# Graph attention on one core: last slots shared by two tiles, one sum moved from TensorE to VectorE, norm constants on GpSimd, unit waits handed to SyncE

## The chip, the cores and the metric

The kernel runs on one core of a Trainium2 chip. The metric is device time in microseconds (us) of one execution; the median of three runs of the kernel before is 1606.07 us (1604.77 to 1610.32). The engines are named as in the profile: PE (TensorE matmul; PEld its weight loads), DVE (VectorE), ACT (ScalarE), POOL (GpSimd) and SP (SyncE, which here only issues DMAs and waits). Each engine works through its own instructions strictly in program order.

## The reference

The inputs are `x` (16 batches of 1024 rows of 512, float32), one adjacency matrix `adj` of 1024 x 1024 for all batches (sparse, with a full diagonal, a few rows much denser than the rest), and weights and biases for q, k and v.

```
h = relu(layernorm(x))                      # mean, variance over 512, eps 1e-5
q, k, v = h @ Wq + bq, h @ Wk + bk, h @ Wv + bv     # 8 heads of 64
scores = einsum(q, k) / 8 ; scores = -1e9 where adj == 0
out = x + softmax(scores) @ v               # per head
```

Only pairs with `adj != 0` matter, and the kernel computes only those.

## The kernel before

**Set-up.** The rows of the adjacency are counted, ranked by degree, and sorted into eight tiles of 128 rows: tile 0 holds the rows with most neighbours, tile 7 those with fewest. For each row the list of its neighbours is made once. Tile t has `CAPS = (11, 8, 6, 5, 4, 3, 3, 2)[t]` slots, so every row of a tile is given as many neighbours as the fullest row of that tile may have; empty places point at a row of zeros. What does not fit into tile 0's slots is spread over a helper tile -1 of 4 slots ("pieces").

**A batch.** For each of the 16 batches: load the eight x tiles in sorted order (`load_x`, POOL), statistics (`stats`, DVE), normalize (`norm`, ACT), transpose (`flip`, PE; `unflip`, ACT), project to k and v (`proj_kv`, PE), copy out of PSUM (`evict_kv`, ACT, half of the v by DVE), store to DRAM (`store_kv`, SP). One `kvt` buffer holds k and v of one tile until its store; there are four. Then the attention: `queries` (PE) projects q of a tile into one of two PSUM buffers; for each slot a `gather` fetches k and v of 128 neighbours, 512 KB (POOL by an indirect DMA; the row's own k and v by SP). The gathered slots live in a ring of 23 places.

**Units.** Slots of a tile are handled in units of 2 to 4 (`PARTS`): 14 units and 46 slots per batch. Per unit: `multiply` (DVE, k times q, L1360), `score` (DVE, sum over each head's 64, L1364), `exponent` (ACT, L1368), weighting of v, most slots by ACT with eight 64-column instructions each (`weigh_s`, L1394), nine slots per batch by DVE (`weigh_v`, L1380), `fold` and `join` (adding the slots of a unit, and units of a tile, DVE L1399 and L1406, some folds by POOL). For tile 0 two matmuls per batch add up what is left (`add_up`, L1418): the pieces by the matrix `owner_t`, the other slots' sum by the identity. Then `row_sums`, `scale`, `residual`, `put_out`. `seen` (L1447) checks each batch's row sums.

**Norm constants.** For each pair of tiles: `variance` (DVE, adds eps, L1080), `power` (POOL, to the power -1/2, L1083), `shift` (DVE, -mean times that, L1087); `norm` waits for `shift`.

**What sets the order.** All instructions are placed by a table of numbers (`PLACES`, one number per step and kind of batch, plus `PERIOD` times the batch); `Plan.ordered` emits them by these numbers, each engine's list in that order. Projections of batch b+1 run on PE beside the attention of batch b. The last batch (b = 15) has rules of its own: there PE adds up nearly all slots.

Of the kernel before, what the change touches and what calls it, by code (L numbers as in the profile page):

```python
# [10 lines left out]
F32 = mybir.dt.float32  # L11
# [7 lines left out]
H = 8  # L19
# [34 lines left out]
SLOTS = sum(n for _, _, n in UNITS) + len(CAPS) + 1  # L54
NU = len(UNITS)
NT = len(CAPS)
BY_VECTOR = {2: 1, 3: 0, 4: 1}
ONE_MORE = ((2, 0),)
LAST_BY_VECTOR = {(2, 0): 0, (2, 3): 0, (0, 0): 0, (-1, 0): 0, (3, 0): 0, (1, 4): 0}
VECTOR_RESIDUAL = (4,)  # L60
LAST_VECTOR_RESIDUAL = (5, 4, 6, 7)
PERIOD = 95.290021
PLACES = {
    'once': dict(
        zeros=(-16.2,),
# [36 lines left out]
        spread_bias=(68.07,),
        copy_bias=(89.7,),
    ),
    'first': dict(
        load_x=(75.29, 75.49, 76.69, 76.89, 78.69, 78.89, 79.29, 79.49,),
        stats=(75.49, 75.69, 76.49, 76.69, 78.89, 79.09, 81.29, 81.49,),
        norm=(75.49, 76.09, 77.09, 77.49, 79.89, 80.09, 80.34, 80.69,),
        flip=(75.49, 75.69, 76.49, 76.69, 78.69, 78.89, 90.39, 104.64,),
        unflip=(75.89, 76.49, 77.29, 77.89, 80.49, 80.72, 96.22, 97.88,),  # L110
        proj_kv=(75.89, 77.49, 76.29, 77.89, 76.89, 78.49, 79.09, 79.29, 86.87, 98.15, 99.79, 107.75, 135.06, 147.6,
            153, 148.32,),
        evict_kv=(76.89, 79.29, 77.69, 79.49, 78.09, 80.29, 80.4, 80.66, 96.1, 96.13, 96.42, 106.28, 154.55, 162.49,
            169.71, 172.46,),
        store_kv=(78.35, 116.17, 119.38, 125.35, 140.7, 146.55, 148.18, 147.06,),
        variance=(75.89, 76.89, 79.29, 81.69,),
# [1553 lines left out]
```

## Time and profile before

| | |
|---|---|
| median of the timed runs | 1606.07 us |
| profiled execution, first to last instruction (its span) | 1595.8 us; the page gives no other time of this execution, and the median lies 10.3 us above the span |
| PE, DVE, ACT, POOL busy | 97%, 96%, 90%, 79% of the span |
| granted PE clock | 0.991 of full on average |
| DMA | 531.55 MB, mean 333 GB/s; 608 gathers by POOL, 128 by SP |
| idle of POOL put down to "issue" | gathers 159.7 us, loads of x 27.6, stores of the output 24.4 |

How to read it: four engines are busy most of the time, so a single busy share does not tell which of them sets the pace. PE's matmuls are pipelined: a matmul of 512 columns shows 592 ns, but the next begins 429 ns later, so PE's real load is read from starts, and from the idle that the profile shows before its instructions. POOL's DMA issues are followed by about 0.3 us in which POOL waits for nothing that the profile shows ("issue").

### The profile page before, as it was taken

How to read it: one execution, taken by the hardware profiler on the slowest of the kernel's cores; microseconds unless marked ns; L12 is line 12 of the kernel's file. 1: busy time of each engine (PE TensorE's matmuls, PEld its weight loads, DVE VectorE, ACT ScalarE, POOL GpSimd, SP SyncE). 2: the span in 40 equal slices, each digit the busy share in tenths (PEclk: the TensorE clock that was granted, in tenths of full speed). 3: DMA queues.
4: the chain of work that ended last, by engine and by line, in shares of the span. 5: the costliest groups of instructions: out<-in, count | busy, mean ns of one | idle time of the engine just before them, and what ended most of it. 6: DMA issues, size and time to landing. Idle time of an engine off the chain costs nothing.

```text
span 1595.8 us, 19282 instructions
## 1 busy us (share of the span) xinstructions
PE 1548.5 (97%) x4151; PEld 719.2 (45%) x4182; DVE 1532.9 (96%) x2105; ACT 1437.5 (90%) x5428; POOL 1257.0 (79%) x1185
## 2 busy tenths in 40 slices
PE   8999999999999999999999999999999999999877
PEld 4444444444444444444444444444444444444333
DVE  8879999999999999999999999999999999999997
ACT  4359989889999999999999999999999998998997
POOL 3767788887888888888888888888888878876775
PEclk9999999999999999999999999999999999999989
DMA  6498989998999999999999999999999999988994
GB/s 251 141 356 308 323 331 347 343 344 323 320 376 340 371 333 337 344 346 375 335 354 343 352 340 342 373 347 372 326 357 339 342 368 328 364 338 295 333 376 191
DMA packets 149875, 531.55 MB, mean 333 GB/s; under 512 B 19052, under 2 KB 19052, under 8 KB 149752
## 3 DMA queue, kind: packets, MB, share of 16 engines
q0 software_dynamic: 109840, 390.70, 67.2%
q1 hardware_dynamic: 39912, 139.56, 23.7%
q8 instruction: 35, 0.57, 0.1%
q14 instruction: 88, 0.72, 0.1%
HBM read 429.46 MB, written 100.72 MB: 332 GB/s over the span
## 4 chain that ended last, share of the span: by engine, by line
DVE 39%; PE 22%; ACT 12%; POOL 10%; issue 9%; DMA 7%; DVEq 0%; POOLq 0%; SPq 0%; ACTq 0%
DVE ring L1360 11%; DVE weights L1364 10%; ACT ring L1394 9%; DVE ring L1399 6%; DMA ring<-kv,index 6%; PE pk L1117 5%; PE pv L1117 5%; PE pq L1117 5%; POOL ring L1350 4%; DVE ring L1380 3%; DVE st L1071 2%; PE pv_first L1117 2%; PE pk_first L1117 2%; POOL ring L1399 2%; POOL x L1062 1%
## 5 line engine op out<-in xcount | busy, mean ns | idle before, releaser
L1394 ACT ACTIVATE ring<-ring,weights 128x64 f32<-128x64 f32 x4704 | 1154.6, 343 | 43.4 <-DVE weights L1373 42.4
L1350 POOL DMA_INDIRECT ring<-kv,index x608 | 618.0, 1016 | 185.5 <-issue 159.7
L1117 PE MATMUL pq<-wq,hT 128*128 128x512 f32 x1024 | 460.3, 592 | 0.8
L1117 PE MATMUL pv<-wv,hT 128*128 128x512 f32 x960 | 433.2, 594 | 3.5 <-ACT kvt L1135 3.3
L1117 PE MATMUL pk<-wk,hT 128*128 128x512 f32 x960 | 433.2, 594 | 1.9 <-ACT hT L1109 1.2
L1364 DVE TENSOR_REDUCE weights<-ring 128x32 f32<-128x2048 f32 (+2 forms) x224 | 422.2, 1890 | 0.9
L1360 DVE TENSOR_TENSOR ring<-ring,pq 128x1536 f32<-128x1536 f32 (+2 forms) x208 | 388.7, 1869 | 4.6 <-DMA ring<-kv,index 4.0
L1117 PEld LDWEIGHTS pq<-wq,hT 128*128 128x128 f32 x1024 | 194.5, 190 | 215.0 <-issue 211.1
L1117 PEld LDWEIGHTS pv<-wv,hT 128*128 128x128 f32 x960 | 182.1, 191 | 227.1 <-issue 216.4
L1117 PEld LDWEIGHTS pk<-wk,hT 128*128 128x128 f32 x960 | 182.7, 191 | 211.0 <-issue 200.6
L1399 DVE TENSOR_TENSOR ring<-ring 128x512 f32<-128x512 f32 (+1 forms) x301 | 253.0, 856 | 2.7 <-ACT ring L1394 2.1
L1471 POOL DMA_INDIRECT out_dram<-x,perm x128 | 151.3, 1182 | 38.1 <-issue 24.4
L1062 POOL DMA_INDIRECT x<-in_x_dram,perm x128 | 142.3, 1111 | 34.0 <-issue 27.6
L1399 POOL TENSOR_TENSOR ring<-ring 128x512 f32<-128x512 f32 x90 | 116.1, 1299 | 10.0 <-DVE ring L1399 8.3
L1380 DVE TENSOR_TENSOR ring<-ring,weights 128x512 f32<-128x512 f32 x143 | 105.8, 747 | 1.3 <-ACT weights L1368 1.0
L1097 ACT ACTIVATE h<-x,shift,rstd 128x512 f32<-128x512 f32 x120 | 94.0, 814 | 0.9 <-DVE shift L1087 0.9
L1468 POOL TENSOR_TENSOR x<-x,o 128x512 f32<-128x512 f32 x64 | 82.4, 1288 | 15.3 <-DVE o L1454 12.7
L1104 PEld LDWEIGHTS pht<-ident,h 128*128 128x128 f32 x512 | 61.9, 141 | 55.6 <-issue 47.8
L1368 ACT ACTIVATE weights<-weights 128x32 f32<-128x32 f32 (+2 forms) x224 | 48.8, 223 | 42.0 <-DVE weights L1364 41.2
L1071 DVE BATCH_NORM_STATS2 st<-x 128x6 f32<-128x512 f32 x120 | 81.2, 677 | 0.1
L1135 ACT COPY kvt<-pk 128x512 f32<-128x512 f32 x120 | 69.4, 578 | 7.8 <-PE pk L1117 7.8
L1104 PE MATMUL pht<-ident,h 128*128 128x128 f32 x512 | 72.7, 274 | 2.7 <-ACT h L1097 2.7
(240 smaller groups left out, 1088.0 us busy)
## 6 DMA issues: line engine op xcount, KB each, us to landing
ring<-kv SPq DMA_DIRECT2D x128, 512.0 KB, 6.7
kv<-kvt SPq DMA_DIRECT2D x120, 512.0 KB, 6.5
ring<-kv,index POOLq DMA_INDIRECT x608, 7.0
ring<-in_adj_dram SPq DMA_DIRECT2D x8, 512.0 KB, 8.2
x_first<-in_x_dram SPq DMA_DIRECT2D x8, 256.0 KB, 6.0
x<-in_x_dram,perm POOLq DMA_INDIRECT x128, 6.1
out_dram<-x,perm POOLq DMA_INDIRECT x128, 5.8
wk<-in_L_gnn_Wk_dram SPq DMA_DIRECT2D x1, 1024.0 KB
```

The lines of the kernel that those rows point to most:

```text
L1062: nc.gpsimd.indirect_dma_start(out=X[n][:], out_offset=None, in_=x_rows, in_offset=on(ap=perm[:, t : t + 1], axis=0), element_offset=b * N * D
L1071: nc.vector.bn_stats(st, X[n])
L1097: nc.scalar.activation(HN[n], X[n], AF.Relu, bias=shift, scale=scale)
L1104: nc.tensor.transpose(PH[n][:, c, :], hn[:, ts(c, P)], ident)
L1117: nc.tensor.matmul(pt, HT[n][:, c, :], W[name][:, c, :], start=(apart and c == 0), stop=(n != -NT and c == DC - 1))
L1350: nc.gpsimd.indirect_dma_start(out=G[i][:, s].rearrange("p j d -> p (j d)"), out_offset=None, in_=KV[b % len(KV)][:], in_offset=on(ap=inde ...
L1360: nc.vector.tensor_tensor(k, k, Q[b, t][:, None, :].to_broadcast([P, count, D]), ALU.mult)
L1364: nc.vector.tensor_reduce(weights[:, w, :], heads(G[i][:, :count, 0, :]), AX.X, ALU.add)
L1380: nc.vector.tensor_tensor(v, v, own.to_broadcast([P, n, H, HD]), ALU.mult)
L1394: nc.scalar.activation(v[:, h, :], v[:, h, :], AF.Identity, scale=weights[:, c + s, h : h + 1])
L1399: engine.tensor_tensor(v[:, 0:n], v[:, 0:n], v[:, first : first + n], ALU.add)
L1471: nc.gpsimd.indirect_dma_start(out=out_rows[t], out_offset=on(ap=perm[:, t : t + 1], axis=0), in_=X.pop(b * NT + TILES.index(t))[:], in_of ...
```

## The change

1. *Shared last slots* (`SHARED`). Tiles 3 and 2 share the last slot (rows 0 to 63 of the slot serve tile 2, the rest tile 3), and tiles 1 and 0 share one (rows 0 to 95 serve tile 0). Rows in tiles 3 and 1 are ranked in reverse so that the fullest rows lie in the half that the slot serves. A batch has 44 slots in 13 units instead of 46 in 14; the ring has 22 places. A shared slot needs a mixed q (`mix`, three ACT copies more per batch), its own `multiply_m`, two small ACT copies of its weights per slot (`halves`), and two half-height adds (`fold_m`, `join_m`).
2. *Tile 0's last sum by VectorE* (`join_acc`). In batches 0 to 14 PE adds up only the pieces; DVE adds that PSUM result to the rest. One `add_up` call per batch goes.
3. *Norm constants on GpSimd.* `variance` and `shift` leave DVE; `power` becomes four POOL instructions.
4. *Row sums checked for five batches* of the sixteen (`SEEN`), each check covering all batches since the last one.
5. *SyncE waits* (`landed`). A SyncE no-op waits for all gathers of a unit and for its q; `multiply` then waits for that no-op alone.
6. The table of places and the lists of who weighs and folds what are new.

```diff
-    3: ((3, 0, 3), (3, 3, 2)),
-    2: ((2, 0, 3), (2, 3, 3)),
+    3: ((3, 0, 5),),
+    2: ((2, 0, 3), (2, 3, 2)),
     1: ((1, 0, 4), (1, 4, 4)),
-    0: ((0, 0, 4), (-1, 0, 4), (0, 4, 4), (0, 8, 3)),
+    0: ((0, 0, 4), (-1, 0, 4), (0, 4, 4), (0, 8, 2)),
+SHARED = {3: (2, 64), 1: (0, 96)}
+SEEN = (4, 9, 13, 14, 15)
-PERIOD = 95.290021
+PERIOD = 93.3
-RING = 23
+RING = 22
...
         def power(m):
+            RSTD[m] = made(m, scale_at, "rstd")
+            SHIFT[m] = made(m, shift_at, "shift")
+            nc.gpsimd.tensor_scalar(RSTD[m], MV[m][:, :, 1], EPS, None, op0=ALU.add)
             nc.gpsimd.tensor_tensor(RSTD[m], RSTD[m], minus_half.to_broadcast(...), ALU.pow)
+            nc.gpsimd.tensor_scalar(SHIFT[m], MV.pop(m)[:, :, 0], -1.0, None, op0=ALU.mult)
+            nc.gpsimd.tensor_tensor(SHIFT[m], SHIFT[m], RSTD[m], ALU.mult)
...
+        add(("landed", k), "SP", slots[:m] + [q_of[q]])
+        add(("multiply", k), "DVE", [("landed", k)], [q])
...
+        def landed(i):
+            b, t, w, c, count = unit(i)
+            LANDED[i] = nc.sync.nop()
+            for made in (*SENT[i], MADE[b, t]):
+                tc.add_manual_dep(LANDED[i].ins, made.ins.name, waits(), reason="the rows of a unit")
...
+        def multiply_m(i):
+            k = GM[i][:, 0, :]
+            nc.vector.tensor_tensor(k, k, QM[i // NU, UNITS[i % NU][0]], ALU.mult)
...
+        def join_acc(b):
+            v = G[b * NU + parts_of(0)[-1]][:, 0, 1, :]
+            nc.vector.tensor_tensor(v, v, ACC.pop((b, 0)), ALU.add)
```

PE, where batch 8's attention ends and batch 9's begins (`acc_0` is tile 0's sum of batch 8, `p_more` the pieces' row sums, `pq_7` to `pq_5` the q of batch 9's tiles 7 to 5, `pk_6` batch 10's k). Before:

```order
L1433 MATMUL p_more_8003<-more_7965,owner_t 128x8
L1418 MATMUL acc_0_8032<-ring,owner_t 128x512
L1115 LDWEIGHTS chosen
L1115 MATMUL pq_6_8035<-bias_parts,chosen 128x512
L1117 MATMUL pq_6_8035<-wq,hT_6_7129 128x512 x4
L1115 LDWEIGHTS chosen
L1115 MATMUL pq_5_8042<-bias_parts,chosen 128x512
L1117 MATMUL pq_5_8042<-wq,hT_5_7380 128x512 x4
L1115 LDWEIGHTS chosen
L1115 MATMUL pk_6_8069<-bias_parts,chosen 128x512
L1117 MATMUL pk_6_8069<-wk,hT_6_7928 128x512 x4
L1418 MATMUL acc_0_8032<-ring,ident 128x512
```

and now, from the last v projection of batch 9 (`pv_0`) on; `pv_7` and `pk_7` are batch 10's:

```order
L1262 MATMUL pv_0_7919<-wv,hT_0_7857 128x512 x4
L1262 MATMUL pv_7_7928<-wv,hT_7_7913 128x512 x4
L1260 LDWEIGHTS chosen
L1260 MATMUL pk_7_7953<-bias_parts,chosen 128x512
L1262 MATMUL pk_7_7953<-wk,hT_7_7913 128x512 x4
L1260 LDWEIGHTS chosen
L1260 MATMUL pq_7_8039<-bias_parts,chosen 128x512
L1262 MATMUL pq_7_8039<-wq,hT_7_7111 128x512 x4
```

```order
L1260 LDWEIGHTS chosen
L1260 MATMUL pv_6_8067<-bias_parts,chosen 128x512
L1262 MATMUL pv_6_8067<-wv,hT_6_7933 128x512 x4
L1662 MATMUL p_more_8089<-more_8034,owner_t 128x8
L1648 MATMUL acc_0_8121<-ring,owner_t 128x512
L1260 LDWEIGHTS chosen
```

The sum by the identity is gone from PE. The v and k projections of tile 7 of batch 10 stand between batch 9's last v and its q of tile 7, which takes the PSUM buffer that tile 0's q of batch 8 held.

SP, the stores of batch 9's k and v (`kvt_1` is tile 1's; the no-ops have no row of their own, their waits stand at the DMA behind them). Before:

```order
L1348 DMA ring<-kv_144 128x1024 [waits DMAHW7_49,DVE_49]
L1159 DMA kv_142<-kvt_4_7549 128x1024 [waits DMAHW6_49,Activation_49]
L1159 DMA kv_142<-kvt_3_7660 128x1024 [waits DVE_49,Activation_49]
L1159 DMA kv_142<-kvt_2_7739 128x1024 [waits DMAHW0_49,Activation_49]
L1159 DMA kv_142<-kvt_1_7798 128x1024 [waits DMAHW1_49,DVE_49,Activation_49]
```

and now:

```order
L1305 DMA kv_145<-kvt_2_7772 128x1024 [waits DMAHW7_49,Activation_49]
L1305 DMA kv_145<-kvt_1_7850 128x1024 [waits DMASW6_49,DMAHW5_49,DMASW4_49,PE_49,DMASW0_49,DMASW5_49,DMASW7_49,DMASW3_49,DMAHW0_49,DVE_49,Activation_49]
L1305 DMA kv_145<-kvt_3_7714 128x1024 [waits DMASW7_49,DMASW6_49,DMASW1_49,DMASW2_49,DMAHW1_49]
L1305 DMA kv_145<-kvt_0_7926 128x1024 [waits DMAHW2_49,Activation_49]
L1527 DMA ring<-kv_145 128x1024 [waits DMASW3_49,DMASW4_49,DMAHW3_49,DMAHW4_49,Pool_49]
```

SP now waits for the gathers (DMASW) of tile 0's first units ahead of the store of tile 1 and for those of its third unit ahead of tile 3's; the no-op of the last unit of batch 8 stands behind the store of tile 0 of batch 9.

POOL, the constants of a pair of tiles of batch 10 (`rstd`). Before:

```order
L1350 DMA ring<-kv_144,index 128x1024 x4
L1083 TENSOR_TENSOR rstd_7620<-rstd_7620,minus_half 128x2
L1350 DMA ring<-kv_144,index 128x1024 x5
L1083 TENSOR_TENSOR rstd_7716<-rstd_7716,minus_half 128x2
L1350 DMA ring<-kv_144,index 128x1024
L1468 TENSOR_TENSOR x_3_6319<-x_3_6319,o_3_7682 128x512
```

and now:

```order
L1530 DMA ring<-kv_147,index 128x1024 x3
L1706 DMA out_dram<-x_4_6359,perm 16384x512
L1530 DMA ring<-kv_147,index 128x1024 x2
L1225 TENSOR_SCALAR rstd_7820<-mv_7705 128x2
L1226 TENSOR_TENSOR rstd_7820<-rstd_7820,minus_half 128x2
L1227 TENSOR_SCALAR shift_7821<-mv_7705 128x2
L1228 TENSOR_TENSOR shift_7821<-shift_7821,rstd_7820 128x2
```

One instruction per pair has become four, in the same place between gathers.

## Rows read from the trace of the kernel before

**Rows 1.** The page: span, and busy time of each engine.
```profile
span 1595.8 us, 19282 instructions
PE 1548.5 (97%) x4151; PEld 719.2 (45%) x4182; DVE 1532.9 (96%) x2105; ACT 1437.5 (90%) x5428; POOL 1257.0 (79%) x1185
```
**Rows 2.** Windows: stretch, length, busy by engine (x), PE clock, DMA share, GB/s.
```profile
100.00:400.00 300.00, 291.37 (x787) 134.69 (x790) 292.71 (x389) 270.96 (x1030) 232.30 (x214) 1.00 0.92 334
600.00:1346.24 746.24, 743.82 (x2000) 346.76 (x2015) 729.10 (x949) 707.61 (x2706) 618.38 (x569) 1.00 0.95 349
1500.00:1560.00 60.00, 45.03 (x100) 18.72 (x100) 58.90 (x56) 56.58 (x239) 46.12 (x46) 0.86 0.96 358
```
**Rows 3.** Timeline of PE around 804 us: start, length, engine, line, instruction.
```profile
804.05 0.38 PE L1115 MATMUL pk<-bias_parts,chosen 128*128 128x512 bf16 x1
804.27 3.60 PE L1117 MATMUL pk<-wk,hT 128*128 128x512 f32 x8
807.70 0.38 PE L1115 MATMUL pk<-bias_parts,chosen 128*128 128x512 bf16 x1
```
**Rows 4.** Groups, PE, 600 to 1346.24: count, busy, mean ns, idle before.
```profile
L1418 PE MATMUL acc<-ring,ident 128*128 128x512 f32 x16 | 8.2, 592 | 0.0
```
**Rows 5.** Groups by shape, DVE, same stretch.
```profile
L1364 DVE TENSOR_REDUCE weights<-ring 128x32 f32<-128x2048 f32 x48 | 109.0, 2270 | 0.0
L1360 DVE TENSOR_TENSOR ring<-ring,pq 128x2048 f32<-128x2048 f32 x40 | 91.2, 2279 | 0.5 <-PE pq L1117 0.3
L1360 DVE TENSOR_TENSOR ring<-ring,pq 128x1536 f32<-128x1536 f32 x48 | 83.8, 1746 | 0.0
L1364 DVE TENSOR_REDUCE weights<-ring 128x24 f32<-128x1536 f32 x48 | 83.4, 1738 | 0.2
L1399 DVE TENSOR_TENSOR ring<-ring 128x512 f32<-128x512 f32 x112 | 73.5, 680 | 0.3
...
L1087 DVE SCALAR_TENSOR_TENSOR shift<-mv,rstd 128x2 f32<-128x2 f32 x32 | 7.4, 230 | 3.2 <-POOL rstd L1083 3.2
L1080 DVE TENSOR_SCALAR rstd<-mv 128x2 f32<-128x2 f32 x32 | 6.4, 200 | 0.0
```
**Rows 6.** Groups by shape, POOL, same stretch.
```profile
L1350 POOL DMA_INDIRECT ring<-kv,index x304 | 308.2, 1014 | 85.2 <-issue 81.9 <-DMA ring<-kv,index 0.9 <-DMA x<-in_x_dram,perm 0.9
L1471 POOL DMA_INDIRECT out_dram<-x,perm x64 | 78.8, 1231 | 18.4 <-issue 12.9 <-POOL x L1468 2.5 <-POOL ring L1399 1.3
L1062 POOL DMA_INDIRECT x<-in_x_dram,perm x65 | 75.6, 1162 | 15.2 <-issue 14.1 <-DMA ring<-kv 1.0
L1399 POOL TENSOR_TENSOR ring<-ring 128x512 f32<-128x512 f32 x48 | 61.1, 1283 | 0.9
...
L1083 POOL TENSOR_TENSOR rstd<-rstd,minus_half 128x2 f32<-128x2 f32 x32 | 23.7, 741 | 4.7 <-DVE rstd L1080 2.9 <-DMA kv<-kvt 1.2
```
**Rows 7.** Groups, POOL, whole span: its smallest copy and iota.
```profile
L927 POOL COPY before_told<-place 128x8 f32<-128x8 f32 x1 | 0.2, 192 | 0.0
...
L917 POOL IOTA place<- 128x8 f32 x1 | 0.1, 136 | 0.0
```
**Rows 8.** Timeline of POOL around 927 us.
```profile
926.64 0.97 POOL L1350 DMA_INDIRECT ring<-kv,index  x1 [0.30 <-issue]
927.92 2.08 POOL L1471 DMA_INDIRECT out_dram<-x,perm  x1 [0.30 <-issue]
```
**Rows 9.** Timeline of DVE at 927.9 us.
```profile
927.91 1.22 DVE L1399 TENSOR_TENSOR ring<-ring 128x1024 f32<-128x1024 f32 x1
```
**Rows 10.** Groups by shape, ACT, 600 to 1346.24.
```profile
L1394 ACT ACTIVATE ring<-ring,weights 128x64 f32<-128x64 f32 x2363 | 580.0, 345 | 26.1 <-DVE weights L1373 25.9
...
L1341 ACT COPY q<-pq 128x512 f32<-128x512 f32 x8 | 4.7, 582 | 0.0
L1368 ACT ACTIVATE weights<-weights 128x16 f32<-128x16 f32 x16 | 3.3, 207 | 0.0
```
**Rows 11.** Timeline around 805 us: ACT weighting two slots, SP storing k and v.
```profile
804.94 3.93 ACT L1394 ACTIVATE ring<-ring,weights 128x64 f32<-128x64 f32 x16
...
809.37 0.32 SPq L1159 DMA_DIRECT2D kv<-kvt  x1
```

More of the change, by code (lines that the diff above doesn't have):

```diff
@@ L104 @@
+        slots=(132.928,),
+        add_bias=(-7.83, 37.133,),
+        spread_bias=(83.593,),
+        copy_bias=(94.282,),
     ),
     'first': dict(
[L106 to L110, printed above, removed]
@@ L382 @@
+POOLS = {'x': 16, 'h': 2, 'pht': 2, 'hT': 11, 'pkv': 2, 'kvt': 4, 'q': 2, 'q0': 1, 'qm': 1, 'acc': 2, 'o': 1}
+RING = 22
 JUNK, SCRATCH, ROWS, LONG_ROWS = NT, NT + 3, NT + 6, NT + 9
 GROUP = 2
+SEEN = (4, 9, 13, 14, 15)
+SUMS_KEPT = 10
 BIAS_V = {0: 'DVE', 2: 'DVE', 4: 'DVE', 6: 'DVE'}
-PAIRED = {10: 12, 12: 13}
-BY_UNIT = ("gather", "multiply", "score", "exponent", "weigh_v", "weigh_p", "weigh_s", "fold", "join", "add_up", "share")
+PAIRED = {9: 11, 11: 12}
+BY_TENSOR = False
+LANDED = True
+BY_UNIT = (
+    "landed", "gather", "multiply", "multiply_m", "score", "exponent", "halves", "weigh_v", "weigh_p", "weigh_s", "fold", "fold_m", "join", "join_m",
+    "add_up", "add_m", "share",
+)
@@ L468, in ordered @@
                 new = [use for use in self.ops[i][3] if use not in has]
-                if all(k in made for k in known[i]) and all(given[use[0]] == at[use] for use in new):
+                if all(k in made for k in known[i]) and all(
+                    given[use[0]] == at[use] and not left.get(before.get(use), 0) for use in new
+                ):
                     ready.append((place[i], i, new))
@@ L524, in planned @@
         add(("list_of", t), "DVE", [("ends",), ("no_diagonal", t)])
-        add(("tell", t), "POOL", [("ranks",), ("shift", (t - NT) // 2)])
+        add(("tell", t), "POOL", [("ranks",), ("power", (t - NT) // 2)])
         add(("spread", t), "POOL", [("list_of", t)])
@@ L556, in planned @@
         if b and k == size - 1:
-            add(("variance", m), "DVE", [("stats", n - k) for k in range(size)])
-            add(("power", m), "POOL", [("variance", m)])
-            add(("shift", m), "DVE", [("power", m)])
-        add(("norm", n), "ACT", [("shift", m) if b else ("load_x", n)], [("x", n), ("h", n)])
+            add(("power", m), "POOL", [("stats", n - k) for k in range(size)])
+        add(("norm", n), "ACT", [("power", m) if b else ("load_x", n)], [("x", n), ("h", n)])
         add(("flip", n), "PE", [("norm", n)], [("h", n), ("pht", n)])
@@ L627, in planned @@
         add(("exponent", k), "ACT", [("score", k)])
+        if m is not None:
+            add(("halves", k), "ACT", [("exponent", k)])
         weights = ("exponent", k)
@@ L695, in planned @@
             add(sums, "DVE", exps, [] if home else [("acc", b, "more")])
-            add(("scale", b, home), "DVE", [sums] + added, [o] if without_tensor(b, B, home) else [acc, o])
-            if without_tensor(b, B, home):
-                touch(first, [0], ("scale", b, home))
+            in_slot = without_tensor(b, B, home) or added[0][0] == "join_acc"
+            add(("scale", b, home), "DVE", [sums] + added, [o] if in_slot else [acc, o])
+            if in_slot:
+                touch(first if without_tensor(b, B, home) else k, [0], ("scale", b, home))
             add(("residual", b, home), by, [("scale", b, home)], [o, x])
             add(("put_out", b, home), "POOL", [("residual", b, home)], [x])
+    for k in range(NU, units):
+        for name in ("score", "halves"):
+            if (name, k) in plan.number:
+                i = plan.number[name, k]
+                key, engine, known, uses = plan.ops[i]
+                plan.ops[i] = key, engine, [*known, *readers_of(plan, k - NU, name)], uses
     bases, held = ring_of(B), before_units()
```

863 lines of the change are left out of this document (520 added, 343 removed), and 36 rows, old and new, of the table gather.

## The prediction

> **What bounds the kernel now.** I read the busy shares of the page first [rows 1]: PE 97% and DVE 96% of the span, ACT 90%, POOL 79%. Shares alone choose nothing, so next come the windows [rows 2]. In the long steady stretch from 600 to 1346.24 us PE is busy 743.8 of 746.2 us. The stretch holds eight batches (32 norm constants at four per batch [rows 6]), so a batch takes 93.28 us and PE is busy 92.98 of it. Is a busy PE a full PE? The timeline [rows 3] says yes: bias plus eight matmuls of one projection run from 804.05 to 807.70, 3.65 us, and the next begins at once; eight matmuls are 3.43 us of it, 0.429 us from start to start although each shows 0.59. The granted clock is 1.00 there [rows 2], the upper of the two levels, 2.4 GHz. So PE sets the pace of the steady part, with 0.3 us per batch idle.
>
> The others stand close behind. DVE is busy 729.1/8 = 91.1 us per batch, ACT 707.6/8 = 88.5 [rows 2]. POOL looks idle at 618.4/8 = 77.3 but is not: the groups by shape [rows 6] put 81.9 + 12.9 + 14.1 = 108.9 us of its idle down to "issue", the pause that follows each DMA it sends, and so POOL's load is (618.4 + 108.9)/8 = 90.9 us. Nothing here has more than 5 us of slack per batch.
>
> Two stretches are not PE's: from 100 to 400 us DVE is busy 292.7 of 300 while PE idles 8.6 us, and from 1500 to 1560, with projections almost done, DVE is busy 58.9 of 60 and PE 45.0 [rows 2]. There DVE ends last.
>
> **The change, part by part.** The sum is made against the span, 1595.8 us; the median of the timed runs is 10.3 us above it, and I add that at the end.
>
> *Tile 0's last sum.* PE loses one `add_up` by the identity per batch. It shows as two matmuls (16 in eight batches [rows 4]), 2 x 0.429 = 0.86 us on the engine that sets the pace, in 15 batches: 12.9 us. DVE gets one 512-column add instead of one join, nothing net. This is the core of the forecast, if PE stays the bound.
>
> *Two slots less.* DVE: a multiply of 2048 columns takes 2.279, one of 1536 1.746 us [rows 5], so 0.533 per slot and 0.147 fixed; a score 0.532 and 0.142. Plain slots fall from 46 to 42 and units by one, and two `multiply_m` of 512 columns come at 0.68 each (as the fold of that width): -4 x 0.533 - 0.147 + 1.36 = -0.92. Scores: two slots and a unit less, -1.21. Folds and joins: four 512-column folds go, four half-height adds come; I price them alike (no row shows a 64-partition add; between half of 0.68 and 0.68). ACT: 2363 weighting instructions take 580.0 us, 0.245 each [rows 10], so two slots of eight are -3.93 and one exponent -0.21; three q copies at 0.582 and four tiny copies at up to 0.207 come: -1.6 net. POOL: two gathers, -2 x (1.014 + 0.30) = -2.63, and one fold more, +1.28 [rows 6].
>
> *Norm constants.* DVE loses four times 0.200 + 0.230 = 1.72 us [rows 5]. DVE's load thus goes from 91.1 to 87.2. POOL gets twelve instructions of two columns per batch. No row shows such a one. From below: its iota of 8 columns, 0.136 us [rows 7], 1.6 us per batch; they can't be a gain, as POOL runs nothing in their place. From above: the power on the same two columns, 0.741 [rows 6], 8.9 us. I take 0.16, between the iota and the copy of 8 columns at 0.192, since a plain add or multiply is nearer to a copy than to a power: 1.9 us. POOL's load becomes 90.9 - 2.6 + 1.3 + 1.9 = 91.5 (91.2 to 98.5).
>
> *What POOL's number hides.* Two neighbouring DMAs of POOL took 0.97 and 2.08 us [rows 8]. The long one began 0.01 us after a DVE fold of 1.22 us, which reads two operands from the ring [rows 9]; it ended 0.87 us after the fold did. POOL's DMA had waited for it. The Trainium skill ("SBUF — State Buffer", Who interferes with whom) says that a VectorE instruction with two SBUF inputs contends with a GpSimd instruction that reads SBUF; the row agrees for an indirect DMA, which reads its index there. By that rule `multiply_m`, with both inputs in SBUF, is a new obstacle, where `multiply` with q in PSUM is none. The number of such DVE instructions per batch barely changes (four folds and a join go, four adds and two `multiply_m` come, and tile 0's `scale` now reads the ring), but which DMA meets which is new with the order. One more meeting with a long fold per batch costs 1.1 us.
>
> *The pace.* PE's floor is 92.98 - 0.86 = 92.1; with the old idle of 0.3, 92.4. POOL at 91.5 fits below by 0.9 us, less than one such meeting, so I charge 0.2 us per batch for it: 92.6 instead of 93.28, -0.66 x 15 = -9.9 us.
>
> *Checks of row sums, SyncE's waits.* The checks take DVE time which is covered by PE's pace: 0. `multiply` waits for one semaphore instead of several; DVE idles 17.1/8 = 2.1 us per batch in all [rows 2], the most that could come back, and it is off the bound: 0. The cost side of the SyncE waits is a rival below. If PE's cover went, both would be gains.
>
> *Start and end.* From 100 to 400 us DVE does 3.9 us less in each of three batches; of PE's 8.6 idle us I take 3 back (0 to 6). At the end DVE has 0.92 + 1.21 us less in the last batch: -2. The set-up gains some seven tiny DVE steps between ranks and lists at about 0.2 each (as the constants above): +1.4.
>
> Sum: -9.9 - 3 - 2 + 1.4 = -13.5, so a span of 1582.3 and a time of 1592.6 us.
>
> **Rivals.**
>
> *POOL becomes the bound.* For it: 0.9 us of room, twelve new instructions, a new set of meetings. Against it: two gathers less, and less waiting for DVE, which has slack now. If a tiny instruction costs 0.30 instead of 0.16, POOL stands at 93.2, and with 0.3 of idle the period is 93.5: +0.2 x 15 = 3.3, with -3.6 at start and end 1605.8 us, no change. The Trainium skill ("GPSIMD Engine Reference", Engine selection) advises VectorE for elementwise work, GpSimd being about twice as slow on two inputs; the folds agree, 1.28 against 0.68 us. By it DVE's 1.72 us would be 3.4 on POOL, the period about 93.3 and the time this rival's.
>
> *SyncE ties DVE to the projections: slower.* The no-op of tile 0's last unit stands behind the store of tile 0's k and v of the next batch. That store waits for ACT to evict the last v; only then may DVE multiply that unit and free the q buffer that PE wants for tile 7. PE covers this with two projections, 3.43 + 3.65 = 7.1 us [rows 3]. The chain: an ACT run of two weighted slots ahead of the eviction, 3.93 [rows 11], the eviction 0.58 (as the q copy [rows 10]), the store's issue 0.32 [rows 11], a DVE score in progress 2.27 [rows 5], a multiply of two slots 1.21 (0.147 + 2 x 0.533): 8.3 us, 1.2 beyond the cover. With two such ACT runs it is 12.2, 5.1 beyond. At the middle, 3.2 us per batch, the period is 92.6 + 3.2 = 95.8: +2.5 x 15 = 38, less 3.6: 1640 us. From about 1.2 us per batch on it is slower than before. Against it: ACT is lighter by 1.6 us per batch, and evictions and DVE instructions are rarely at their worst together.
>
> *Everything runs at PE's floor.* Lighter DVE, ACT and DMA take PE's idle too: 92.1 per batch, -1.18 x 15 = -17.7, start -6, end -2, set-up +1.4: -24.3, 1582 us. Against it: POOL.
>
> **How the numbers follow.** Forecast 45% (1592.6, its own range 1584 to 1601), POOL the bound 24% (1598 to 1612), SyncE's chain 18% (1605 and up), PE's floor 13% (1578 to 1585). About 0.3%, 4.8 us, is what a measurement of this kernel tells from no change: 1601.2 to 1610.9. Faster: nearly all of the forecast, the floor, and a third of POOL's, 0.44 + 0.13 + 0.08 = 0.65. Same: 0.15, most of POOL's and a little of the others. Slower: 0.20, nearly all of SyncE's and a bit of POOL's. The range, 1580 to 1612, leaves out a little of the floor's case and most of SyncE's.
>
> **What would show it.** In the steady stretch of the new profile: a period near 92.6 us; PE still over 99% busy and one `acc` matmul pair per batch; DVE's load near 87, its idle between 4 and 6 us; the POOL instructions on two columns at 0.14 to 0.2 us, and POOL's busy time plus issue near 91.5. If POOL's DMAs stand closer together and PE idles before q projections or weights for gathered rows, POOL is the bound. If PE idles 1 us or more before `pq` of tile 7 while DVE waits for SP, the chain through SyncE is real. A start or an end that differs by more than 6 us would make the sum wrong though the period is right.

## The result, and the profile after

The changed kernel takes 1737.66 us (median; 1734.33 to 1740.09), the kernel before 1606.23 beside it: a ratio of 1.0816, 95% interval 1.0796 to 1.0836. I had forecast 1592.6 us and a range of 1580 to 1612. It is slower by 8.2%, outside the range and on the other side of no change.

The page of the changed kernel, span and busy times, beside [rows 1]:

```profile
span 1736.8 us, 19246 instructions
PE 1589.2 (91%) x4152; PEld 728.4 (42%) x4152; DVE 1533.8 (88%) x1969; ACT 1425.6 (82%) x5268; POOL 1334.3 (77%) x1360
```

DVE's busy time is unchanged, ACT's is less, PE's and POOL's are more. The shares of PE, DVE and ACT fell by 6 to 8 points, POOL's by 2: the engines wait for each other. Windows of the changed kernel (columns as in [rows 2]):

```profile
100.00:400.00 300.00, 278.63 (x746) 128.41 (x745) 264.94 (x350) 241.80 (x883) 216.91 (x229) 0.98 0.83 293
600.00:1400.00 800.00, 748.58 (x1969) 344.59 (x1968) 723.35 (x866) 692.57 (x2590) 651.83 (x643) 0.97 0.87 308
1500.00:1560.00 60.00, 54.65 (x151) 25.30 (x151) 55.05 (x64) 48.23 (x177) 44.78 (x48) 1.00 0.87 307
```

In the long stretch PE was busy all but 0.3% before; now it lacks 51.4 of 800 us. How long is a batch? One DVE instruction, `more`, occurs once in each. Timeline of DVE, batches 3 and 13, first of the changed kernel, then of the kernel before:

```profile
513.69 0.22 DVE L1658 TENSOR_REDUCE more<-weights 128x8 f32<-128x40 f32 x1
1533.09 0.23 DVE L1658 TENSOR_REDUCE more<-weights 128x8 f32<-128x40 f32 x1
```
```profile
474.52 0.21 DVE L1429 TENSOR_REDUCE more<-weights 128x8 f32<-128x40 f32 x1
1408.32 0.21 DVE L1429 TENSOR_REDUCE more<-weights 128x8 f32<-128x40 f32 x1
```

Ten batches took 1019.40 us instead of 933.80: a period of 101.94 instead of 93.38. The first `more` stands at 216.5 us instead of 188.6, so 28 us are lost before the steady part begins. Of the 141 us of span, ten steady batches carry 86, the start 28, the other batches and the end the rest. (The medians differ by 131 us only. The changed kernel's profiled run took 1.8 us more than its span; if that held before too, the profiled execution of before was about 9 us quicker than its median, an estimate.)

Where POOL spends its time, groups by shape, 600 to 1400 us, changed kernel (busy us, mean ns, idle before; beside [rows 6]):

```profile
L1530 POOL DMA_INDIRECT ring<-kv,index x282 | 302.3, 1072 | 89.0 <-issue 80.4 <-DVE ring L1627 1.8 <-POOL x L1703 1.3
L1607 POOL TENSOR_TENSOR ring<-ring 128x512 f32<-128x512 f32 x56 | 71.1, 1285 | 0.7
...
L1226 POOL TENSOR_TENSOR rstd<-rstd,minus_half 128x2 f32<-128x2 f32 x31 | 30.7, 992 | 2.6
L1227 POOL TENSOR_SCALAR shift<-mv 128x2 f32<-128x2 f32 x31 | 21.3, 687 | 2.1
L1225 POOL TENSOR_SCALAR rstd<-mv 128x2 f32<-128x2 f32 x31 | 15.7, 506 | 2.3
L1228 POOL TENSOR_TENSOR shift<-shift,rstd 128x2 f32<-128x2 f32 x31 | 11.4, 368 | 2.6
```

The four norm-constant instructions of a pair take 2.55 us together (79.1/31), where the power alone took 0.741 [rows 6]: 7.2 us more per batch. Why is an instruction on two columns so long? Timeline of POOL, then of DVE, same stretch:

```profile
1335.44 1.22 POOL L1225 TENSOR_SCALAR rstd<-mv 128x2 f32<-128x2 f32 x1
1336.75 1.55 POOL L1226 TENSOR_TENSOR rstd<-rstd,minus_half 128x2 f32<-128x2 f32 x1
1338.37 1.89 POOL L1227 TENSOR_SCALAR shift<-mv 128x2 f32<-128x2 f32 x1
```
```profile
1335.35 2.96 DVE L1607 TENSOR_TENSOR ring<-ring 128x1024 f32<-128x1024 f32 x3
1338.35 0.69 DVE L1619 TENSOR_TENSOR ring<-ring 96x512 f32<-96x512 f32 x1
1338.96 1.21 DVE L1607 TENSOR_TENSOR ring<-ring 128x1024 f32<-128x1024 f32 x1
```

DVE is folding, two operands from the ring each time. The adding of eps takes 1.22 us, the power 1.55, the negation 1.89, while DVE runs such folds one after another. Where DVE reduces, or multiplies by a q that lies in PSUM, the same three and the last product were as short as 0.23, 0.72, 0.24 and 0.19 us. POOL, then DVE, 15 us later:

```profile
1350.00 0.23 POOL L1225 TENSOR_SCALAR rstd<-mv 128x2 f32<-128x2 f32 x1
1350.31 0.72 POOL L1226 TENSOR_TENSOR rstd<-rstd,minus_half 128x2 f32<-128x2 f32 x1
```
```profile
1349.03 1.75 DVE L1572 TENSOR_REDUCE weights<-ring 128x24 f32<-128x1536 f32 x1
```

They are not slow, they are held.

What the engines wait for, four large rows of the view of waits, 600 to 1400 us (total us, times, longest):

```profile
ACT h L1242 <- POOL shift L1228: 33.2, 10, 6.1
DVE ring L1556 <- SPq L1543: 30.9, 20, 3.6
PE acc L1648 <- POOL ring L1607: 25.3, 8, 5.7
PE pv L1260 <- DVE kvt L1279: 19.0, 12, 3.4
```

None of the four stands in that list of before; of the older waits, ACT's for DVE's scores grew from 9.3 to 28.1 us. Three of the four have POOL, or what POOL brings, at their root: ACT waits for the norm constants, PE for a POOL fold, DVE for SyncE's no-op, which itself waits for gathers most of the time (350 us of SyncE's waits at it in the same stretch, behind its queue). The last is the same chain one step on. Timeline of DVE, then of PE, near 908 us:

```profile
906.49 2.29 DVE L1556 TENSOR_TENSOR ring<-ring,pq_-1_7009 128x2048 f32<-128x2048 f32 x1 [1.59 <-SPq L1543]
908.69 0.68 DVE L1279 TENSOR_TENSOR kvt<-pv,bias_rows 128x512 f32<-128x512 f32 x1
```
```profile
909.43 0.59 PE L1260 MATMUL pv<-bias_parts,chosen 128*128 128x512 bf16 x1 [3.45 <-DVE kvt L1279]
909.81 6.75 PE L1262 MATMUL pv<-wv,hT 128*128 128x512 f32 x9
```

A multiply waits 1.59 us for the no-op; behind it on DVE stands the copy of v that empties PE's PSUM buffer; so PE waits 3.45 us. Then its next matmuls are slow. Windows around it:

```profile
896.00:908.00 12.00, 9.91 (x29) 4.34 (x28) 8.57 (x7) 10.47 (x37) 9.81 (x10) 1.00 1.01 394
908.00:915.00 7.00, 5.57 (x8) 2.38 (x8) 6.97 (x5) 4.44 (x16) 6.07 (x7) 0.53 0.92 326
915.00:925.00 10.00, 10.00 (x26) 4.47 (x25) 8.17 (x14) 8.77 (x36) 4.80 (x6) 0.99 0.99 355
```

The granted clock is 0.53 after the wait, the lower level (1.2 of 2.4 GHz), and 0.99 again from 915 on. The nine matmuls show 6.75 us, where eight showed 3.60 [rows 3]; at 0.429 us from start to start nine would have shown about 4.0, an estimate, so some 2.7 us come on top of the 3.45. The wait is paid almost twice.

### The profile page after: what moved, and what is told of

Read it like the earlier page. It is cut to its first block, busy times and chain, and to the rows that moved or that the text cites. A ratio compares the mean times of both kernels' runs of the same rounds, so it can differ in the third digit from the quotient of the medians.

```text
span 1736.8 us, 19246 instructions
## 1 busy us (share of the span) xinstructions
PE 1589.2 (91%) x4152; PEld 728.4 (42%) x4152; DVE 1533.8 (88%) x1969; ACT 1425.6 (82%) x5268; POOL 1334.3 (77%) x1360
## 5 line engine op out<-in xcount | busy, mean ns | idle before, releaser
L1602 ACT ACTIVATE ring<-ring,weights 128x64 f32<-128x64 f32 x4448 | 1093.5, 337 | 15.6 <-DVE weights L1581 12.5
L1262 PE MATMUL pv<-wv,hT 128*128 128x512 f32 x960 | 446.0, 611 | 6.8 <-issue 3.7
L1556 DVE TENSOR_TENSOR ring<-ring,pq 128x1536 f32<-128x1536 f32 (+2 forms) x192 | 350.9, 1833 | 86.1 <-SPq L1543 33.1
L1572 DVE TENSOR_REDUCE weights<-ring 128x32 f32<-128x2048 f32 (+3 forms) x208 | 404.5, 1947 | 1.9
L1607 DVE TENSOR_TENSOR ring<-ring 128x512 f32<-128x512 f32 (+1 forms) x241 | 223.6, 936 | 5.3 <-ACT ring L1602 3.4
L1203 POOL DMA_INDIRECT x<-in_x_dram,perm x128 | 131.0, 1023 | 50.2 <-issue 28.5
L1706 POOL DMA_INDIRECT out_dram<-x,perm x128 | 134.5, 1051 | 40.2 <-issue 30.4
L1607 POOL TENSOR_TENSOR ring<-ring 128x512 f32<-128x512 f32 x105 | 136.1, 1309 | 5.9 <-ACT ring L1602 1.8
L1576 ACT ACTIVATE weights<-weights 128x32 f32<-128x32 f32 (+3 forms) x208 | 45.8, 221 | 81.1 <-DVE weights L1572 79.2
L1254 ACT COPY hT<-pht 128x512 f32<-128x512 f32 x128 | 72.9, 572 | 18.6 <-PE pht L1249 9.9
```

The costliest lines, as they stand in the source:

```text
L1203: nc.gpsimd.indirect_dma_start(out=X[n][:], out_offset=None, in_=x_rows, in_offset=on(ap=perm[:, t : t + 1], axis=0), element_offset=b * N * D
L1262: made = nc.tensor.matmul(pt, HT[n][:, c, :], W[name][:, c, :], start=(apart and c == 0), stop=(n != -NT and c == DC - 1))
L1556: product = nc.vector.tensor_tensor(k, k, Q[b, t][:, None, :].to_broadcast([P, count, D]), ALU.mult)
L1572: waited(nc.vector.tensor_reduce(weights[:, w, :], heads(G[i][:, :count, 0, :]), AX.X, ALU.add), i)
L1602: nc.scalar.activation(v[:, h, :], v[:, h, :], AF.Identity, scale=weights[:, c + s, h : h + 1])
L1607: added = engine.tensor_tensor(v[:, 0:n], v[:, 0:n], v[:, first : first + n], ALU.add)
```

## The experiments

All times are against the kernel before, run beside it on the same chip; rows with the same time of before share a chip. "Hold-ups" are the time of DVE and POOL instructions above the undisturbed length (10th percentile) of their own kind (line, operation, names and shape), per batch, worked out from all rows between the `more` of batch 4 and of batch 13: 8.8 us in the kernel before (DVE 2.1, POOL 6.8), 14.9 after (4.2 and 10.7). (The expectation of p0 below speaks of 8.0 and 12.0 for the kernel before and for r0; by this count they are 8.8 and 13.8.) The theories: **A** norm constants on GpSimd; **B** SyncE's no-ops; **C** the new order of the work; **D** the additional work of shared slots; **E** the meetings of DVE and POOL that an order makes. (c5, c6, b3 and b4 ran on a chip where the kernel before took 0.9% longer, so that their periods compare with the others' only to about that.)

| kernel | time | before | ratio (95%) | period | first `more` |
|---|---|---|---|---|---|
| changed kernel | 1737.66 | 1606.23 | 1.0816 (1.0796, 1.0836) | 101.94 | 216.5 |
| c1_norm_back | 1688.06 | 1600.23 | 1.0559 (1.0536, 1.0582) | 98.32 | 203.6 |
| c2_no_landed | 1725.35 | 1600.23 | 1.0775 (1.0757, 1.0793) | 101.33 | 206.4 |
| b1_norm_pool | 1674.81 | 1600.23 | 1.0464 (1.0446, 1.0481) | 99.94 | 189.1 |
| d3_two_more | 1767.30 | 1600.23 | 1.1056 (1.1028, 1.1085) | 104.48 | 206.1 |
| c5_shift_early | 1699.74 | 1614.86 | 1.0531 (1.0505, 1.0556) | 98.27 | 216.3 |
| c6_no_landed | 1709.03 | 1614.86 | 1.0587 (1.0561, 1.0612) | 98.65 | 216.9 |
| b3_join_acc | 1615.05 | 1614.86 | 1.0006 (0.9990, 1.0022) | 94.28 | 193.6 |
| b4_landed | 1620.29 | 1614.86 | 1.0035 (1.0020, 1.0050) | 94.05 | 192.3 |
| r0_before_reordered | 1698.14 | 1600.47 | 1.0613 (1.0582, 1.0643) | 97.65 | 209.7 |
| r1_back_reordered | 1712.15 | 1600.47 | 1.0694 (1.0674, 1.0714) | 101.25 | 199.5 |
| r2_after_reordered | 1701.69 | 1600.47 | 1.0631 (1.0610, 1.0651) | 99.70 | 202.8 |
| p0_before_turns | 1632.54 | 1600.61 | 1.0205 (1.0188, 1.0222) | 94.66 | 209.5 |
| p1_back_turns | 1669.77 | 1600.61 | 1.0434 (1.0417, 1.0452) | 96.71 | 211.5 |
| p2_after_turns | 1729.40 | 1600.61 | 1.0809 (1.0790, 1.0827) | 101.50 | 207.3 |
| n1_no_shared_adds | 1658.59 | 1601.64 | 1.0350 (1.0333, 1.0367) | 96.34 | 203.5 |
| h2_before_new_order | 1804.19 | 1604.91 | 1.1235 (1.1207, 1.1264) | 105.18 | 216.7 |
| h3_fold_earlier | 1768.13 | 1609.10 | 1.0995 (1.0956, 1.1033) | 102.11 | 214.4 |

**The norm constants (A).** *c1_norm_back*: the changed kernel with variance and shift on DVE again.

```diff
-            add(("power", m), "POOL", [("stats", n - k) for k in range(size)])
+            add(("variance", m), "DVE", [("stats", n - k) for k in range(size)])
+            add(("power", m), "POOL", [("variance", m)])
+            add(("shift", m), "DVE", [("power", m)])
...
```

> The changed kernel, with the norm constants as they were: VectorE adds eps and multiplies by the mean, GpSimd makes only the power; each of VectorE's two stands in its order where the trace of the changed kernel had it when the power ended. Theory A (GpSimd sets the pace, since the constants hold it for 2.55 us a pair of tiles where the power alone took 0.74): 4 x 1.8 = 7.2 us of a period of 101.9 go, over some 14 batches 100 us: 1635 us, between 1610 and 1650, and with the excess of the first 200 us (28 us) still there. Theory B (the chain through SyncE sets it): 1738 less a few: over 1725. Theory C (the new table of places is at fault): over 1700.

1.0559: 2.6% (41 us) come back, a third of the loss. That is less than half of the 100 us that A expected, and more than B or C allowed. *b1_norm_pool* is the reverse: the kernel before, where `power` makes all four instructions on `nc.gpsimd`.

> The kernel before with one part of the change alone: all four instructions of the norm constants on GpSimd. Theory A: GpSimd's load of 91.9 us of 93.3 grows by 7.2 to 99.1, so the period grows by 5 to 7 us and the whole by 70 to 100: 1690 us, between 1670 and 1715. Theories B and C: this part is harmless, 1595 to 1620.

1.0464: alone in the kernel before they cost 4.6%, so A is shown, from both sides. The four groups of norm constants on POOL in b1, 600 to 1400 us:

```profile
L1083 POOL TENSOR_TENSOR rstd<-rstd,minus_half 128x2 f32<-128x2 f32 x32 | 24.9, 777 | 2.7
L1084 POOL TENSOR_SCALAR shift<-mv 128x2 f32<-128x2 f32 x32 | 10.7, 334 | 2.2
L1082 POOL TENSOR_SCALAR rstd<-mv 128x2 f32<-128x2 f32 x32 | 10.6, 332 | 2.4
L1085 POOL TENSOR_TENSOR shift<-shift,rstd 128x2 f32<-128x2 f32 x32 | 7.9, 248 | 2.7
```

Here a small instruction costs 0.25 to 0.33 us and 0.08 of idle before it. POOL is busy 82.9 us per batch and pauses 15.7 (gaps up to 0.32 us): 98.6 of a period of 99.9. In the old order POOL became the bound outright.

*d3_two_more*: the changed kernel with the adding of eps made three times.

```diff
             nc.gpsimd.tensor_scalar(RSTD[m], MV[m][:, :, 1], EPS, None, op0=ALU.add)
+            nc.gpsimd.tensor_scalar(RSTD[m], MV[m][:, :, 1], EPS, None, op0=ALU.add)
+            nc.gpsimd.tensor_scalar(RSTD[m], MV[m][:, :, 1], EPS, None, op0=ALU.add)
```

> The changed kernel with the sum of variance and eps made three times instead of once (eight small instructions more on GpSimd a batch, nothing else). Theory A: each costs its mean of 0.51 us and a gap of 0.08: 4.7 us a batch, over 14 batches 66 us: 1800 us, between 1770 and 1815. Theory B or C: GpSimd has slack, 1730 to 1750.

1.1056, 2.4% (38 us) above the changed kernel: 8 instructions in 16 batches, 0.30 us each. At the 1606 us of the first comparison that is 1776, inside A's range at its lower end; POOL is still on the path.

*c5_shift_early* asks whether c1's remainder lies in where I had put DVE's shift: one or two instructions earlier.

> c1_norm_back with one thing moved: VectorE's product of mean and power stands one or two instructions earlier in its order, where the trace of c1_norm_back had it when the power ended. In that trace ScalarE's normalization waits 53 us of 800 behind VectorE's order (DMA of rows 29.3, share 12.4, shift 6.5, row sums 5.3), 6.6 us a batch. Theory A2 (with GpSimd relieved, what is left above the kernel before is this wait): ratio 1.025 to 1.04. Theory C (the new order as a whole costs the rest): 1.05 or more, as c1_norm_back's 1.056.

1.0531, the same as c1 within the intervals. It doesn't.

**SyncE's waits (B).** *c2_no_landed* is the changed kernel without the no-ops, *c6_no_landed* c5 without them, *b4_landed* the kernel before with them.

```diff
-        add(("landed", k), "SP", slots[:m] + [q_of[q]])
-        add(("multiply", k), "DVE", [("landed", k)], [q])
+        add(("multiply", k), "DVE", slots[:m] + [q_of[q]], [q])
...
```

> The changed kernel without SyncE's empty instructions: each multiplication waits for its rows and its queries itself. Theory A (GpSimd): rows still come late, VectorE waits for them as long: 1738, between 1720 and 1745. Theory B (SyncE): the wait of 1.5 us and more a unit at the empty instruction goes, and with it 4 to 8 us a batch: under 1680.

> c5_shift_early without SyncE's empty instructions. Theory B (SyncE's chain costs once GpSimd doesn't hide it): 1.0% or more below c5_shift_early. Theory A: the same within 0.5%, as on the changed kernel itself (0.4% there).

> The kernel before with one part alone: SyncE's empty instruction ahead of each multiplication, in SyncE's order where the trace of before has the multiplication. The prediction's step (hidden: rows lie ready): 0.998 to 1.003. Theory B (the chain of SyncE, the prediction's rival of 1640): 1.01 to 1.025.

Without them 0.4% less (c2, as A expected), without them 0.6% more (c6, where B expected 1% less and A no change), with them 0.35% more (b4, just above the 1.003 of the prediction's step and well below B's 1.01). Of my three rivals this was the one that I thought slower; it is hardly there, and its sign depends on the rest.

*b3_join_acc*: the kernel before with tile 0's last sum on DVE.

> The kernel before with one part alone: the last sum of tile 0 by VectorE (0.64 us a batch on VectorE more, 0.65 us on TensorE less). The prediction's step (TensorE sets the pace): 0.65 x 14 = 9 us faster, ratio 0.994. If VectorE, with 92.6 of 93.4 us, is as much the bound: 1.000 to 1.006.

1.0006, outside the 0.994 that the pace of PE would give: the 0.86 us per batch that PE is spared bring nothing, even in the old order. DVE gets an add more here (0.68 us), and PE now waits for DVE before its q projections, for 10.3 us of 800 in several rows (1.4 in the kernel before). The largest of them:

```profile
PE pq L1127 <- DVE ring L1372: 6.0, 6, 1.4
```

So DVE stood as close to the pace as PE.

**The order, first attempts (C).** What is left of c1 and c5, 5.3 to 5.6%, is shared slots or the new order. *r1*, *r2* and *r0* give c5, the changed kernel and, as a control, the kernel before an order made anew, from durations read in the trace; `places` returns one number per step and no instruction changes.

```diff
     def places(self):
-        ...
+        return ORDER
```

> c5_shift_early (the whole change but for the norm constants, which VectorE and GpSimd make as before), its instructions and their work the same, with every engine's order made anew: each instruction is put where it became ready when the engines' queues are followed through with the durations measured in that kernel's trace. Theory C (the new table of places, not the shared slots, costs the 5.3%): at least 3% of it goes, ratio 1.00 to 1.025. Theory D (the shared slots' own instructions on VectorE, ScalarE and GpSimd cost it, whatever the order): 1.04 to 1.06.

> The changed kernel itself, norm constants on GpSimd, with every engine's order made anew in the same way. Theory A and C together (GpSimd sets the pace with a load of 96 to 99 us a batch, and the order adds to it): 1.045 to 1.065, between the changed kernel's 1.082 and b1_norm_pool's 1.046. Theory A alone: 1.075 or more. If only the order counted: 1.02 or less.

> The kernel before with every engine's order made anew in the same way, as a control: no instruction is changed. If making an order in this way gains or loses little by itself: 0.99 to 1.015.

The control failed: 1.0613 where I expected about 1. So r1, above both of its theories' ranges, and r2 can't say what shared slots are worth. But they show what I hadn't meant to ask. The same instructions in another order cost 6% (r0). The changed kernel gets 1.7% faster by a new order alone (r2: 1.0631 against 1.0816), so at least that much of its loss is its own order's. And between r1 and r2, each in an order of its own, the norm constants have the other sign: on GpSimd they are 0.6% better; why, I haven't traced. Windows, then groups of DVE, 600 to 1400 us, of r0:

```profile
600.00:1400.00 800.00, 767.58 (x2050) 354.69 (x2065) 785.06 (x971) 728.79 (x2785) 635.29 (x581) 1.00 0.91 335
```
```profile
L1286 DVE TENSOR_SCALAR rstd<-mv 128x2 f32<-128x2 f32 x32 | 16.2, 506 | 0.2
L1293 DVE SCALAR_TENSOR_TENSOR shift<-mv,rstd 128x2 f32<-128x2 f32 x33 | 15.3, 463 | 0.0
L1579 DVE TENSOR_TENSOR weights<-weights,inv 128x24 f32<-128x24 f32 x16 | 11.5, 718 | 0.3
```

DVE is busy 785 of 800 us: here it is the bound, with the instructions of the kernel before. The adding of eps takes 0.506 us where it took 0.200 [rows 5], the shift 0.463 instead of 0.230. Timeline of POOL, then of DVE, in r0:

```profile
747.07 1.27 POOL L1674 TENSOR_TENSOR x<-x,ring 128x512 f32<-128x512 f32 x1 [0.71 <-DVE ring L1605]
```
```profile
747.38 1.00 DVE L1579 TENSOR_TENSOR weights<-weights,inv 128x24 f32<-128x24 f32 x1
```

A product of 24 columns begins 0.31 us into POOL's residual add and ends with it. It happens in almost the same place in each batch, since the order is the same in each. The adding of eps, with one operand in SBUF, is held too: it takes 0.13 to 0.29 us in most rows, but 1.50 to 1.56 in the one per batch beside which POOL folds. DVE, then POOL:

```profile
922.94 1.55 DVE L1286 TENSOR_SCALAR rstd<-mv 128x2 f32<-128x2 f32 x1
```
```profile
923.16 1.27 POOL L1605 TENSOR_TENSOR ring<-ring 128x512 f32<-128x512 f32 x1
```

So meetings go both ways: POOL's instructions are held by DVE's, and DVE's by POOL's. Hold-ups in r0 are 13.8 us per batch (before: 8.8), 6.7 of them on DVE.

**The order, searched for fewer meetings (E).** *p1*, *p2* and *p0* (c5, the changed kernel, the kernel before) start from each kernel's own order and try small moves, counting the time in which DVE and POOL hold each other.

> c5_shift_early (all of the change but the norm constants), its instructions the same, the order searched by small moves from its own, this time with two things that the traces show and r1_back_reordered left out: a VectorE instruction with two operands in SBUF and a GpSimd add or small instruction wait for each other, and a GpSimd DMA that starts beside such a VectorE instruction ends 0.83 us after it. Theory E (the missing 5% is these two engines meeting, and what waits for them): 2 to 3% of it goes, ratio 1.02 to 1.035. Theory D (the shared slots' instructions themselves): 1.045 to 1.06.

> The changed kernel, norm constants on GpSimd, order searched in the same way from its own. Theory E: 3% of its 8.2 goes, 1.04 to 1.055, below r2_after_reordered (1.063), which had ready times alone. If the meetings don't count: 1.06 to 1.08.

> Control: the kernel before, order searched in the same way from its own. It has few meetings to lose (8.0 us a batch in all above the undisturbed durations, where r0_before_reordered has 12.0): 0.99 to 1.01, where r0_before_reordered stands at 1.061.

p1 gains 1% on c5, between the two theories' ranges; p2 gains nothing, though E gave it 3%; and the control lost 2%. Hold-ups in p0 fell a little, to 8.3 us per batch, and its period rose by 1.3, so meetings are not all that an order decides. The search also made p0's start 21 us later.

**The shared slots (D).** *n1_no_shared_adds* is c5 without the six DVE instructions per batch that only shared slots need. It leaves the products of shared slots out of the scores and their values out of the sums.

```diff
-            nc.vector.tensor_tensor(k, k, QM[i // NU, UNITS[i % NU][0]], ALU.mult)
...
-            nc.vector.tensor_tensor(v, v, GM[i][rows, 1, :], ALU.add)
...
-            nc.vector.tensor_tensor(v, v, GM.pop(i)[rows, 1, :], ALU.add)
+            GM.pop(i)
```

> c5_shift_early without the six VectorE instructions a batch that only the shared slots need (two multiply_m, two fold_m, two join_m: 6 x 0.68 = 4.1 us of VectorE's 94.9 a batch; the products of the shared slots are left out of scores and sums). Theory D (these instructions cost the 5.3%): VectorE's load falls to 90.8, below TensorE's 93: ratio 1.00 to 1.015. Theory C/E (the order, with waits and meetings all over it): the time falls by less than half of that, 1.03 to 1.05.

1.0350: they cost 1.8% of c5, and 3.5% stay with less DVE work than the kernel before has. D alone falls.

**The changed kernel's order under the old instructions (C).** *h2_before_new_order* has all 46 slots and every instruction of the kernel before, each step where the table of the changed kernel has it; what that table lacks stands beside its neighbours (the shifts where c5 has them), and the last batch keeps its numbers. One weighing by DVE passes to tile 2's other unit.

```diff
-PLACES = { ... }    # of before
+PLACES = { ... }    # of the changed kernel, with the fifth unit and two slots filled in
```

> The kernel before with all its 46 slots, 14 units and instructions, but every step that the kernel after has too stands where the table of after puts it; the fifth unit of the old list and the two slots more stand right beside their neighbours, and the last batch's attention keeps the old numbers. F: what is left of the slowdown without the norm constants on GpSimd and the shared slots' six VectorE instructions (3.5%) is the price of the new order. Then this kernel is at 1.03 to 1.06 of before, its first batch's `more` comes at 200 us or later instead of at 188.6, and its period is 95.5 to 98 us. G: the rest lies in what else the shared slots bring (mixed q, copies of halves of weights, other ranks), and the order alone costs little: 0.99 to 1.015, period 93 to 94.5.

1.1235, far above C's own range: dearer than the change itself. Its largest wait, 600 to 1400 us:

```profile
POOL ring L1328 <- DVE ring L1328: 59.0, 8, 7.7
```

POOL stands still 7.4 us per batch before a fold, for one DVE fold whose place I had filled in. *h3_fold_earlier* puts that fold 4 numbers earlier (2 to 4 instructions on DVE) and changes nothing else.

> The run before (the instructions of before in the order of the changed kernel) with one VectorE instruction per batch put earlier: the first fold of tile 1's second unit, for which GpSimd stood still 7.3 us per batch, moves two to four instructions ahead on VectorE; every other instruction keeps its place. F1: that wait was the price of that one place, and the rest of the new order is dear as well: 1.04 to 1.095, with a first batch as late as there (`more` at 205 us or later). F2: the wait only moves to another engine or instruction: 1.11 to 1.13. G: the new order is cheap once that place is mended: below 1.03.

1.0995, 2.4 points less: one instruction per batch, put a few places earlier, is worth 36 us (39 by the two ratios; the two ran on different chips). The result lies 0.5% above F1's range and well below F2's. The same wait in h3, then the first of the others:

```profile
POOL ring L1328 <- DVE ring L1328: 19.2, 8, 3.5
```
```profile
ACT weights L1297 <- DVE weights L1293: 34.0, 19, 2.8
PEld acc L1347 <- ACT hT L1038: 23.0, 7, 3.8
ACT h L1026 <- DVE shift L1016: 22.1, 8, 3.2
POOL ring L1279 <- ACT h L1026: 21.6, 7, 3.2
```

The rest is spread over many places. And the late start comes with the order alone: the first `more` stands at 216.7 and 214.4 us in h2 and h3, as in the changed kernel, with the instructions of before. It isn't peculiar to this order: r0 and p0 start late as well (209.7 and 209.5), and c1 and c5, which differ by the place of one instruction per pair, are 13 us apart. What the new order costs the old instructions beyond the filled-in places can't be read from these two.

**What this adds up to.** Of 8.2%, the norm constants on GpSimd are 2.6 to 2.9 in this order (changed kernel against c1, c5) and the shared slots' six DVE instructions 1.8 (c5 against n1). The no-ops and `join_acc` are within 0.6 either way. The remaining 3.5% go with the new order and whatever else shared slots bring (mixed q, halves of weights, other ranks), which I haven't taken apart. That an order alone can cost as much is shown by r0 and h3 (p0: 2%); that it is this order is shown for 1.7% (r2), and by h2 and h3 for the late start; for the rest it is inferred. No version tried beats the kernel before.

## Why the prediction was wrong, point by point

- **The step that failed first: "Norm constants".** I priced twelve instructions at 0.16 us, 1.9 us per batch, on the ground that "a plain add or multiply is nearer to a copy than to a power". Unhindered they take 0.19 to 0.24 us, 2.6 us for the twelve, so their own size was not far off. In the kernel they take 0.25 to 0.33 (b1) or 0.37 to 0.69, and the power went from 0.741 to 0.99: +7.2 us per batch instead of +1.9, against 2.4 us of slack between POOL's 90.9 and PE's 93.28. The upper bound, 8.9 us for all twelve at the power's price, was the nearer one, by luck: the power is long by its own size (0.72 unhindered), the small ones by the folds that hold them. The warning stood in [rows 8, 9].
- **"What POOL's number hides"** had the mechanism right, and the row [rows 8, 9] that shows it, and then charged 0.2 us per batch. Hold-ups grew by 6.1 us per batch, 4.0 of them on POOL. I counted a meeting with an indirect DMA only, and the DMAs' hold-ups didn't grow (6.5 us per batch before, 6.0 after). POOL's small instructions take part too, each of which can wait for a whole fold: the sixteen of the norm constants lose 4.5 us per batch after, where the four powers lost 0.1 before. The Trainium skill ("SBUF — State Buffer", SBUF: two separate sides) calls the shared ports an exclusive lock, which the instruction that starts first keeps for its whole length. The 1.22 us of adding eps to two columns, and the 1.00 us of r0's product, agree; r0's adding of eps doesn't, which by its row started 0.22 us ahead of POOL's fold and still ended with it.
- **"PE sets the pace", and so the core of the gain.** PE idles 7 us per batch. POOL's busy time and pauses are 83.0 + 14.8 = 97.8 of 101.9 us, nearer to the period than any other engine's, so the rival *POOL becomes the bound* named the right engine, but with 0.30 us per instruction, an unchanged power and no wait passed on to PE, ACT and DVE it came to 1605.8. And b3 says that the gain was not there even in the old order: 1.0006, since PE then waits for DVE.
- **What was not in the sum at all: the new order.** I read the table as a neutral carrier and priced instructions only. "A new set of meetings" stands in one rival, without a price. r0's 6%, p0's 2% and the 36 us of one fold show what it may cost where four engines stand within about 5% of the pace. How much of the 3.5% that stays open is this order, no run says.
- **"Start and end"**: -3 and -2 forecast; the first `more` came 28 us later and the stretch behind the last one was 4 us longer.
- **DVE's load** was to fall to 87 us; it is 92.2. Its hold-ups, 2.1 us more, took about half of the fall of 3.9; the durations of its instructions sum to 1.5 us less per batch. The price of the half-height adds was right, they cost as much as full ones: 0.69 us for 96 partitions, above, and for 32, as 0.68 for 128 [rows 5]. Group of DVE in the changed kernel, 600 to 1400 us:

```profile
L1614 DVE TENSOR_TENSOR ring<-ring 32x512 f32<-32x512 f32 x8 | 5.5, 688 | 0.2
```

- **SyncE's chain**, the slower rival: the wait is real (20 times, 30.9 us), but without the no-ops DVE waits for gathers itself (19 times, 25.7 us in c2, and the time falls by 0.4%). Its sign, PE idle before `pq` of tile 7, is missing: in that stretch PE shows no wait before a q projection.

## What to carry to other kernels

When several engines stand within a few per cent of the pace, price an instruction on GpSimd by the length of the VectorE instructions with two SBUF operands beside which it will run, not by its own size: a two-column add is as long as the fold that holds it, and 0.23 us beside a reduction. Count each engine's load with its pauses, and take a new order of a tuned kernel as a change with a price of its own, of some per cent in either direction, tested alone with the old instructions. And undo parts from the changed side as well as adding them to the old one: the norm constants cost 2.6% there and 4.6% here.

## What the runs showed of the hardware that I had not expected

- A VectorE instruction with two SBUF inputs and a GpSimd add hold each other to the end of the other's instruction, in either direction: 1.00 instead of 0.18 us (DVE, 24 columns), 1.22 instead of 0.23 (POOL, 2 columns). In r0 the DVE instruction of two columns with one SBUF input, the adding of eps, is held as well: 1.55 us beside a POOL fold, 0.13 to 0.29 otherwise.
- After a PE wait of 3.45 us the granted clock fell to the lower level (0.53 on average from 908 to 915), so that nine matmuls showed 6.75 us; in the kernel before it stayed at 1.00 over the whole long stretch [rows 2].
- An add over fewer partitions saves nothing on VectorE: 0.69 us over 96 and over 32 partitions, 0.68 over 128.
